# The experts' up projection with the tokens of both batches in one pass over the weights

## The chip, the core and the metric

The kernel runs on one core of a Trainium2 chip. A core has several engines that run at the same time, each through its own list of instructions in order: TensorE (PE in the profile) for matrix products, VectorE (DVE), ScalarE (ACT) and GpSimdE (POOL) for everything done element by element, and SyncE (SP), which here only starts transfers. Engines wait for each other through semaphores. TensorE works in pairs of instructions: LDWEIGHTS loads a stationary piece of 128 x 128, shown as PEld, and MATMUL streams up to 512 columns past it and adds the result into a PSUM bank. Eight banks of PSUM stand beside the main on-chip memory, SBUF.

The metric is the time of one execution on the device, in microseconds; lower is better.

## The reference

x has 2 batches of 512 tokens with 1024 features. The first part is a residual around a product of the normalized x with a context, both rounded to 256 levels. The second part, which the change touches, is a mixture of experts with a shared gated MLP:

```python
x = x + tanh(g_xattn) * (fake_quant(layernorm(x)) @ fake_quant(ctx))
xt = layernorm(x)
# gate: the two best of 16 experts per token, within the two best of 4 groups
y = 0
for e in experts:
    h = silu(xt @ w1[e] + b1[e]) * (xt @ w2[e] + b2[e])     # 1024 -> 256
    y = y + gate[:, e] * (h @ w3[e] + b3[e])                # 256 -> 1024
z = (silu(xt @ sw1 + sb1) * (xt @ sw2 + sb2)) @ sw3 + sb3   # hidden size 512
x = x + tanh(g_ffn) * (y + z)
```

## The kernel before

Everything is in float32 quality. A large product is made of three products in a faster float32 format (fp32r): each operand is split into a high half (`h` at the end of a name, or XH) and a low half (`l`, or XL), and the result is high x high + high x low + low x high. The token tiles count from t=0 to 7, four for each batch.

The kernel has four stages. In the first, up to about 106 us, x is normalized, quantized, multiplied with the context and normalized again, and transposed into XH and XL; part of the shared MLP's hidden layer is worked in between. This stage is written as a list of steps in a fixed order (START). In the second the rest of the shared hidden layer is made, with the router between its parts. In the third comes the shared down projection. In the fourth, from 200 us on, the two experts that the inputs choose, one after the other, each with an up projection and a down projection. A program that chose more experts would run the others in a loop behind it; that loop is not entered here.

An expert's hidden layer has 256 columns, worked in two blocks `c` of 128 (`expert`, L670). For a block, `load_up` (L308) starts two transfers of 512 KB, for the first and the second matrix (tiles named e0a0r, e0b0r: expert 0, matrix a or b, block 0, raw). `split_up` (L316) makes their halves: ACT copies the raw tile into the high half (L302), and DVE subtracts to get the low half (L304). Then `up` (L342) works on batch 0 and after it on batch 1. `up_mm` (L319) takes one matrix after the other. For a matrix it runs 24 products of 512 columns into one PSUM bank: eight row pieces of the high weights with XH, the same eight with XL, then the eight low pieces with XH. `up_post` (L333) makes the batch's hidden values: ACT's Silu of the first bank (L337), DVE's multiplication with the second (L338), ACT's cast to the high half (L339) and DVE's subtraction for the low half (L340). In the second block the expert's output bias, times the gate, is added to X by DVE in eight instructions (L386), in the program ahead of the block's products.

The down projection (`load_down` L345, `down` L366) loads and splits two tiles of w3 (e0d0r and e0d1r), and then takes the token tiles one after the other. For a tile and a block it runs six products of 512 columns: four with the tile's high hidden piece (high and low weights, for each half of the output columns, L372 and L373) and two with the low hidden piece (L375). DVE adds the result times the gate to X (L378). In the second expert each tile is stored when it is done; the last tile is done and stored in three column pieces (`down_last`).

Outside of START nobody writes the order of the instructions by hand. The framework's planner lays it down when the program is built: it goes through the program with estimated durations, decides on each engine which instruction comes next, and gives each tile a place from its pool. All weights in work, the hidden values and the biases come from one pool of 22 places of 4 KB a partition, PSUM's banks from a pool of six:

```python
slabs = ctx.enter_context(tc.tile_pool(name="slabs", bufs=22))
ps_mm = ctx.enter_context(tc.tile_pool(name="ps_mm", bufs=6, space=bass.MemoryType.PSUM))
```

What the planner laid down is then the fixed order in which each engine works, whatever the real durations are; each transfer is started by SP as soon as its place is free.

Of the kernel before, what the change touches and what calls it, by code (L numbers as in the profile page):

```python
# [19 lines left out]
D = 1024  # L20
KD = D // P
B = 2
# [12 lines left out]

# the order in which the start's loads and steps are issued, each step as function.arguments
LOADS = "x.1 x.3 c.0 c.1 x.2 c.2 c.3 c.4 c.5 c.6 c.7.0 c.7.1 w.1.1 x.4 b w.1.0 w.0.1 x.5 w.0.0"
# [40 lines left out]
def flamingo_block(  # L78
# [3 lines left out]
    nc = tc.nc  # L82
# [19 lines left out]

# [1 line left out]
    sc_in = const.tile([P, 6], F32, name="sc_in")  # L104
    nc.sync.dma_start(sc_in, scal.partition_broadcast(P))

# [1 line left out]
    X = [keep.tile([P, D], F32, name=f"X{t}") for t in range(NT)]  # L108

    # the engine that starts the DMAs; the paths that are rarely taken use GpSimd's queue  # L110
    dq = [nc.sync]
# [5 lines left out]

# [1 line left out]
    mhalf = const.tile([P, 1], F32, name="mhalf")  # L119
# [12 lines left out]
    nc.vector.tensor_scalar(nz, sc_in[:, 0:4], -1.0, None, ALU.mult)  # L132
    # zero points that bf16 holds exactly, less any quantized value, are integers of 0..255
    z8 = const.tile([P, 4], U8, name="z8")
# [25 lines left out]

# [1 line left out]
    def bn(t, h):  # L162
# [49 lines left out]

# [1 line left out]
    c8_, raws, qT, cq, acc = {}, {}, {}, {}, {}  # L214
# [21 lines left out]

# [1 line left out]
    sq_, md_, xn_, px_ = {}, {}, {}, {}  # L238

    def e(t, h):  # L240
        """The residual and its sum."""
        if h == 0:
            sq_[t] = [small.tile([P, 2], F32, name=f"{n}{t}", tag=n, bufs=4) for n in "sq"]
        xs = X[t][:, half(h)]
        nc.vector.scalar_tensor_tensor(  # L245
            xs, acc[t][h], cx_scale, xs, ALU.mult, ALU.add, accum_out=sq_[t][0][:, h : h + 1]
        )

    def sq(t, h):
        """H^2 times the squared deviations from the mean of half a row, H values."""  # L250
        if h == 0:
            xn_[t] = slab(f"xn{t}", F32)
        s, q = sq_[t]
        nc.scalar.activation(  # L254
            xn_[t][:, half(h)], X[t][:, half(h)], AF.Square,
            bias=s[:, h : h + 1], scale=-float(H), accum_out=q[:, h : h + 1],
        )

    def fm(t, eng):
        """The mean, and what the difference of the halves' means adds to the variance."""  # L260
        s, eng = sq_[t][0], pick(eng)
        d = small.tile([P, 1], F32, name=f"d{t}", tag="d", bufs=4)
        eng.tensor_tensor(d, s[:, 0:1], s[:, 1:2], ALU.subtract)
        eng.tensor_scalar(d, d, d, H / 2.0, ALU.mult, ALU.mult)
        nm = small.tile([P, 1], F32, name=f"nm{t}", tag="nm", bufs=4)
        eng.tensor_scalar(nm, s[:, 0:1], s[:, 1:2], -1.0 / D, ALU.add, ALU.mult)
        md_[t] = nm, d
# [38 lines left out]

# [1 line left out]
    def load_up(name, w1, w2, c):  # L308
# [10 lines left out]
    def up_mm(name, c, b, w, lo=0, n=S, i=(0, 1)):  # L319
# [11 lines left out]
        return got  # L331

    def up_post(name, c, b, acc, b1, b2, hid, lo=0, n=S):  # L333
        hh, hl = hid
        out = slice(b * S + lo, b * S + lo + n)
        sa = small.tile([P, S], F32, name=f"{name}sa{c}_{b}_{lo}", tag="w2k", bufs=3)[:, :n]
        nc.scalar.activation(sa, acc[0], AF.Silu, bias=b1)  # L337
        nc.vector.scalar_tensor_tensor(sa, acc[1], b2, sa, ALU.add, ALU.mult)  # L338
        nc.scalar.copy(hh[:, out], sa)  # L339
        nc.vector.tensor_tensor(hl[:, out], sa, hh[:, out].bitcast(F32), ALU.subtract)  # L340
# [12 lines left out]
    def down_last(name, t, hid, w3, scale):  # L353
        """A tile in column pieces, each stored as soon as it is done."""
        n = len(hid)
        for lo, w in ((0, 512), (512, 256), (768, 256)):
            cols = slice(lo, lo + w)
            po = bank(f"{name}po{t}_{lo}")[:, :w]
            for c, ((hh, hl), (wh, wl)) in enumerate(zip(hid, w3)):
                nc.tensor.matmul(po, hh[:, ts(t, P)], wh[:, cols], start=c == 0, stop=False)  # L360
                nc.tensor.matmul(po, hh[:, ts(t, P)], wl[:, cols], start=False, stop=False)
                nc.tensor.matmul(po, hl[:, ts(t, P)], wh[:, cols], start=False, stop=c == n - 1)
            nc.vector.scalar_tensor_tensor(X[t][:, cols], po, scale, X[t][:, cols], ALU.mult, ALU.add)
            dq[0].dma_start(of[ts(t, P), cols], X[t][:, cols])
# [22 lines left out]

    # ================= program =================
    XH, XL = ([keep.tile([P, KD, S], F32R, name=n), None] for n in ("XH0", "XL0"))
# [40 lines left out]

# [1 line left out]
    bT = const.tile([P, NB], F32, name="bT")  # L432
# [5 lines left out]

    # TensorE's clock is low until it has been busy for a few microseconds
    zero = const.tile([P, S], BF16, name="zero")  # L440
# [8 lines left out]

    # biases of the hidden layers, as columns  # L450
    def pb():
# [5 lines left out]

    # shared weights, split: half h of the rows of matrix i, hidden columns c
    def wh(c, i, h, eng):
# [8 lines left out]

    # hidden columns c of tokens lo..lo+255: matrix i, pass p of three
    def um(c, lo, i, p):  # L470
# [38 lines left out]

    # router weights, padded to the columns of a quarter of TensorE, and constants of the router  # L510
    rwf = const.tile([P, KD, QC], F32, name="rwf")
# [15 lines left out]
    def stage(b):  # L527
        """The buffers of a batch's attention."""
        qT[b] = keep.tile([P, TB, KD, P], BF16, name=f"qT{b}", tag="xh1")
        cq[b] = keep.tile([P, KD, D], BF16, name=f"cq{b}", tag="xl1")  # L530
# [12 lines left out]

# [1 line left out]
    def rt(name, shape=(P, NT, E), dtype=F32):  # L545
# [6 lines left out]
    def router_x(b):  # L552
        """The normalized x, transposed, in one float32 piece."""
        xs = []
        for i in range(4):
            x = slab(f"xf{b}_{i}", F32, (P, 2, S))
            nc.gpsimd.tensor_tensor(  # L557
                x, XH[b][:, ts(i, 2)].bitcast(F32), XL[b][:, ts(i, 2)].bitcast(F32), ALU.add
            )
            xs.append(x)  # L560
        return xs

    # the four quarters of TensorE's columns work at the same time, each on a fourth of the rows of D
    def router_logits(b, lT, xs):
# [19 lines left out]
    def first_max(name, v, n):  # L584
        """One-hot of the first largest of the last n."""
        m = rt(f"{name}m", (P, NT))
        nc.vector.tensor_reduce(m, v, AX.X, ALU.max)
        o = rt(f"{name}o", (P, NT, n))
        nc.vector.tensor_tensor(o, v, over(m, n), ALU.is_equal)
        order = tie[:, E - n :].unsqueeze(1).to_broadcast([P, NT, n])  # L590
        nc.vector.tensor_mul(o, o, order)
        nc.vector.tensor_reduce(m, o, AX.X, ALU.max)
        nc.vector.tensor_tensor(o, order, over(m, n), ALU.is_equal)
        return o

    # of all experts some token chose: 16 - e; of the others: 0
    key = route.tile([P, E], F32, name="key")
# [48 lines left out]
    def next_expert(j):  # L646
        """Of the chosen experts left, the one of lowest index: its index, gates and hidden biases."""
        m = rt(f"m{j}", (P, 1))
# [19 lines left out]

# [1 line left out]
    def expert(j, e, gv, bv, store):  # L670
        wc = lambda w: (lambda c: w[ds(e, 1), :, ts(c, P)].rearrange("o (k p) n -> p (o k) n", p=P))
        hid = []
        for c in range(EC):
            w = split_up(f"e{j}", c, load_up(f"e{j}", wc(ew1), wc(ew2), c), nc.vector)
            hid.append(new_hid(f"e{j}h{c}"))
            if c == EC - 1:
                bb = load_bias(f"e{j}", eb3[ds(e, 1), :].rearrange("o d -> (o d)").partition_broadcast(P))
                for t in range(NT):
                    add_bias(t, bb, gv[:, t : t + 1])
            for b in range(B):  # L680
                up(f"e{j}", c, b, w, bv[:, 0, c : c + 1], bv[:, 1, c : c + 1], hid[c])
        w3 = load_down(f"e{j}", lambda c: ew3[ds(e, 1), ts(c, P), :].rearrange("o p d -> (o p) d"), range(EC))
# [20 lines left out]

    # the rest of the shared MLP's hidden layer, with the router in between
    lT = slab("lT", F32)
# [21 lines left out]

# [1 line left out]
    def attention_exact(b):  # L729
# [64 lines left out]

# [1 line left out]
    n_exp = nc.values_load(n_chosen[0:1, 0:1], min_val=2, max_val=E)  # L796
# [54 lines left out]
```

## Time and profile before

| what | value |
|---|---|
| time, median of three runs | 344.21 us (344.01 to 344.89) |
| span of the profiled execution | 342.9 us |
| TensorE, matrix products | 321.7 us busy, 94% of the span, 1673 products |
| TensorE, weight loads | 254.5 us busy, 1673 loads |
| DVE, ACT, POOL | 197.0, 95.4 and 79.0 us busy |
| up projection of an expert | 192 products, 44.98 us |
| down projection of expert 0 | 245 to 267 us |
| bytes moved | 31.45 MB, mean 92 GB/s |

The profile has no total of its own beside the span for the profiled execution; the span runs from the first to the last instruction of the program, and the timed runs are 1.3 us longer at the median. A row of the timeline gives start and length in us, engine, line, operation, the tiles (result first, then operands) and the number of instructions merged in it; in brackets stands how long the engine had been idle before, and what ended the wait. The length of a product is its latency: products overlap, so the rate is read from their starts. "Busy" of TensorE counts that latency too.

### The profile page before, as it was taken

The numbers are of one execution on the slowest core, as the hardware profiler recorded it, in microseconds if no ns is written. First come the engines' busy times: TensorE is split into PE (matmuls) and PEld (weight loads), VectorE is DVE, ScalarE is ACT, GpSimd is POOL, SyncE is SP. The second block draws the span as 40 slices with busy tenths as digits, with TensorE's granted clock in tenths as the row PEclk, the third lists the DMA queues.
The fourth block names the chain that finished last, engine by engine and source line by source line (L and its number), as shares of the span: only waits on it lengthen the run. The fifth ranks groups of instructions, "written<-read, shape, count | busy, mean of one in ns | idle before, by whom it ended". The sixth has DMA issues, their size and how long they took to land.

```text
span 342.9 us, 4322 instructions
## 1 busy us (share of the span) xinstructions
PE 321.7 (94%) x1673; PEld 254.5 (74%) x1673; DVE 197.0 (57%) x335; ACT 95.4 (28%) x148; POOL 79.0 (23%) x110
## 2 busy tenths in 40 slices
PE   6588899989999999999999999999999999999990
PEld 2244886769998686888888888888888888888870
DVE  3879999879723126736754632494484135834560
ACT  2756877672213135120200002112400012030000
POOL 2795798868600740000000000000000000000000
PEclk9899999999999999999999999999999999999997
DMA  6999920000004033101200091201310400001542
GB/s 207 420 375 391 399 62 0 2 0 2 0 2 123 9 118 122 63 0 59 66 0 0 8 329 33 62 2 32 90 61 2 122 0 2 0 0 50 198 183 74
DMA packets 25892, 31.45 MB, mean 92 GB/s; under 512 B 2492, under 2 KB 19204, under 8 KB 25860
## 3 DMA queue, kind: packets, MB, share of 16 engines
q1 hardware_dynamic: 25860, 31.05, 26.5%
q8 instruction: 17, 0.28, 0.3%
q14 instruction: 15, 0.12, 0.1%
HBM read 26.85 MB, written 4.19 MB: 91 GB/s over the span
## 4 chain that ended last, share of the span: by engine, by line
PE 75%; DVE 8%; POOL 5%; ACT 4%; issue 3%; DMA 2%; SPq 0%; DVEq 0%; POOLq 0%
PE sp L327 16%; PE e1p L327 13%; PE e0p L327 13%; PE sp L476 5%; PE spo L373 4%; PE spo L372 4%; PE spo L375 4%; ACT xn L254 2%; PE e0po L372 2%; PE e0po L373 2%; PE e0po L375 2%; PE e1po L373 2%; PE e1po L372 2%; PE e1po L375 2%; DVE xn L283 2%
## 5 line engine op out<-in xcount | busy, mean ns | idle before, releaser
L233 PE MATMUL at<-cq,qT 128*128 128x512 bf16 x128 | 30.3, 379 | 2.5 <-POOL cq L153 1.5
L557 POOL TENSOR_TENSOR xf<-XH,XL 128x1024 f32<-128x1024 f32 x8 | 19.9, 2497 | 22.4 <-PE sp L327 19.6
L233 PEld LDWEIGHTS <-qT 128*128 128x128 bf16 x128 | 12.1, 98 | 15.5 <-issue 2.9
L378 DVE SCALAR_TENSOR_TENSOR X<-spo,tg,X 128x512 f32<-128x512 f32 x16 | 11.3, 746 | 16.0 <-PE spo L375 16.0
L338 DVE SCALAR_TENSOR_TENSOR ssa<-sp,bT,ssa 128x512 f32<-128x512 f32 (+1 forms) x6 | 4.0, 662 | 26.1 <-PE sp L327 26.1
L337 ACT ACTIVATE e0sa<-e0p,bv 128x512 f32<-128x512 f32 x4 | 2.8, 690 | 49.4 <-PE e0p L327 49.4
L378 DVE SCALAR_TENSOR_TENSOR X<-e0po,gv,X 128x512 f32<-128x512 f32 x16 | 11.3, 747 | 7.3 <-PE e0po L375 7.3
L283 DVE TENSOR_SCALAR xn<-X,nm,d 128x512 f32<-128x512 f32 x16 | 13.8, 891 | 1.4 <-POOL d L279 1.3
L378 DVE SCALAR_TENSOR_TENSOR X<-e1po,gv,X 128x512 f32<-128x512 f32 x14 | 9.9, 747 | 8.2 <-PE e1po L375 8.2
L288 PE MATMUL px<-ident,xn 128*128 128x128 f32 x64 | 9.3, 275 | 3.5 <-DVE xn L283 2.3
L337 ACT ACTIVATE e1sa<-e1p,bv 128x512 f32<-128x512 f32 x4 | 2.8, 690 | 34.9 <-PE e1p L327 34.9
L338 DVE SCALAR_TENSOR_TENSOR e1sa<-e1p,bv,e1sa 128x512 f32<-128x512 f32 x4 | 3.0, 752 | 15.9 <-PE e1p L327 15.9
L254 ACT ACTIVATE xn<-X,s 128x512 f32<-128x512 f32 x16 | 11.4, 716 | 1.9 <-DVE X L245 1.4
L245 DVE SCALAR_TENSOR_TENSOR X<-at,cx_scale,X 128x512 f32<-128x512 f32 x16 | 11.6, 742 | 0.1
L165 DVE BATCH_NORM_STATS2 st<-X 128x6 f32<-128x512 f32 x16 | 10.3, 680 | 2.2 <-DMA X<-in_dram 2.2
L338 DVE SCALAR_TENSOR_TENSOR e0sa<-e0p,bv,e0sa 128x512 f32<-128x512 f32 x4 | 3.0, 751 | 14.6 <-PE e0p L327 14.6
L288 PEld LDWEIGHTS px<-ident,xn 128*128 128x128 f32 x64 | 7.2, 141 | 5.6 <-ACT XH L145 2.6
L298 DVE TENSOR_TENSOR XL<-px,XH 128x512 fp32r<-128x512 f32 x16 | 10.4, 679 | 0.8 <-ACT XH L145 0.8
L386 DVE SCALAR_TENSOR_TENSOR X<-sbias,tg,X 128x1024 f32<-128x1024 f32 x8 | 10.3, 1284 | 0.3
L153 POOL TENSOR_SCALAR cq<-q8c,nz 128x1024 bf16<-128x1024 uint8 (+1 forms) x8 | 10.0, 1250 | 1.0 <-DVE q8c L223 0.6
L208 PE MATMUL pq<-ident_b,qx 128*128 128x128 bf16 x64 | 5.4, 228 | 4.7 <-ACT qx L151 4.4
L386 DVE SCALAR_TENSOR_TENSOR X<-e1bias,gv,X 128x1024 f32<-128x1024 f32 x8 | 9.8, 1280 | 0.0
(402 smaller groups left out, 830.9 us busy)
## 6 DMA issues: line engine op xcount, KB each, us to landing
cr<-in_dram SPq DMA_DIRECT2D x15, 512.0 KB, 9.2
out_dram<-X SPq DMA_DIRECT2D x15, 256.0 KB, 2.4
X<-in_dram SPq DMA_DIRECT2D x7, 512.0 KB, 9.0
X<-in_dram SPq DMA_DIRECT2D x2, 256.0 KB, 4.1
cr<-in_dram SPq DMA_DIRECT2D x2, 256.0 KB, 9.1
sb1r<-in_dram SPq DMA_DIRECT2D x1, 512.0 KB, 9.0
sa1r<-in_dram SPq DMA_DIRECT2D x1, 512.0 KB, 7.2
sb0r<-in_dram SPq DMA_DIRECT2D x1, 512.0 KB, 8.2
```

The lines of the kernel that those rows point to most:

```text
L233: nc.tensor.matmul(acc[t][h], qT[b][:, t % TB, k, :], cq[b][:, k, half(h)], start=(k == 0), stop=(k == KD - 1))
L254: nc.scalar.activation(xn_[t][:, half(h)], X[t][:, half(h)], AF.Square, bias=s[:, h : h + 1], scale=-float(H), accum_out=q[:, h : h + 1],)
L283: nc.vector.tensor_scalar(xn_[t][:, half(h)], X[t][:, half(h)], nm, r, ALU.add, ALU.mult)
L288: nc.tensor.transpose(px_[t, q][:, k, :], xn_[t][:, ts(4 * q + k, P)], ident)
L327: nc.tensor.matmul(p, wx[:, k, :], xx[b][:, k, cols], start=first and k == 0, stop=last and k == KD - 1)
L372: nc.tensor.matmul(po[h], hh[:, ts(t, P)], wh[:, ts(h, 512)], start=first, stop=False)
L373: nc.tensor.matmul(po[h], hh[:, ts(t, P)], wl[:, ts(h, 512)], start=False, stop=False)
L375: nc.tensor.matmul(po[h], hl[:, ts(t, P)], wh[:, ts(h, 512)], start=False, stop=last)
L378: nc.vector.scalar_tensor_tensor(xs, po[h], scale, xs, ALU.mult, ALU.add)
L386: nc.vector.scalar_tensor_tensor(X[t], bb, scale, X[t], ALU.mult, ALU.add)
L476: nc.tensor.matmul(up_[c, lo, i], w[:, k, :], x[0][:, k, lo : lo + 256], start=p == 0 and k == 0, stop=p == 2 and k == KD - 1,)
L557: nc.gpsimd.tensor_tensor(x, XH[b][:, ts(i, 2)].bitcast(F32), XL[b][:, ts(i, 2)].bitcast(F32), ALU.add)
```

## The change

Only the experts' up projection changes. A new function `up_both` takes the two matrices in turn. For a matrix it opens two banks, one for each batch, and goes through the eight row pieces once. At each it runs four products with the high weight piece (batch 0 with XH and XL, batch 1 with XH and XL) and then two with the low weight piece (batch 0 and batch 1 with XH). `expert` calls it once for a block and then calls `up_post` for batch 0 and for batch 1. The number of products, loads, banks, transfers and of the instructions in `up_post` stays what it was. The shared MLP keeps `up`. The diff also takes comments away; nothing else differs.

```diff
+    def up_both(name, c, w):
+
+        got = [[], []]
+        for i in range(2):
+            ps = [bank(f"{name}p{c}_{b}_{i}") for b in range(B)]
+            for k in range(KD):
+                for b in range(B):
+                    for j, xx in enumerate((XH, XL)):
+                        nc.tensor.matmul(
+                            ps[b], w[i][0][:, k, :], xx[b][:, k, :], start=k == 0 and j == 0, stop=False
+                        )
+                for b in range(B):
+                    nc.tensor.matmul(ps[b], w[i][1][:, k, :], XH[b][:, k, :], start=False, stop=k == KD - 1)
+            for b in range(B):
+                got[b].append(ps[b])
+        return got
+
...
     def expert(j, e, gv, bv, store):
...
+            both = up_both(f"e{j}", c, w)
             for b in range(B):
-                up(f"e{j}", c, b, w, bv[:, 0, c : c + 1], bv[:, 1, c : c + 1], hid[c])
+                up_post(f"e{j}", c, b, both[b], bv[:, 0, c : c + 1], bv[:, 1, c : c + 1], hid[c])
```

## The prediction

> **What bounds the kernel now.** I read the page's busy rows and its chain first, then the chain in order of time, then TensorE's timeline, and last the timelines of ACT, DVE and the DMA queue around the experts. The page:
>
> ```profile
> span 342.9 us, 4322 instructions
> PE 321.7 (94%) x1673; PEld 254.5 (74%) x1673; DVE 197.0 (57%) x335; ACT 95.4 (28%) x148; POOL 79.0 (23%) x110
> PEclk9899999999999999999999999999999999999997
> PE sp L327 16%; PE e1p L327 13%; PE e0p L327 13%; PE sp L476 5%; PE spo L373 4%; PE spo L372 4%; PE spo L375 4%; ACT xn L254 2%; PE e0po L372 2%; PE e0po L373 2%; PE e0po L375 2%; PE e1po L373 2%; PE e1po L372 2%; PE e1po L375 2%; DVE xn L283 2%
> ```
>
> TensorE sets the time, at the full granted clock, and each expert's up projection (e0p, e1p) is 13% of the chain. Every MATMUL has its own LDWEIGHTS (1673 of each), so a repeated piece is loaded again. The chain in order of time (start and length in us, as in the timelines below) shows both up projections without a gap:
>
> ```profile
> 200.13 44.98 PE e0p L327 x192
> ...
> 266.87 44.98 PE e1p L327 x192
> ```
>
> 44.98 us over 192 products is **234.3 ns** a product. TensorE's timeline of the down projection gives the starts of two tiles that follow each other:
>
> ```profile
> 247.67 0.39 PE L372 MATMUL e0po<-e0d0h,e0h0h 128*128 128x512 f32 x1
> ...
> 250.39 0.39 PE L372 MATMUL e0po<-e0d0h,e0h0h 128*128 128x512 f32 x1
> ```
>
> 12 products in 2.72 us: **226.7 ns** each, for products of the same size and type (the 0.39 is one product's latency, and they overlap).
>
> **The gain.** `up` does eight pieces of the high half with XH, the same eight with XL, then eight low pieces, so the piece changes at every product. `up_both` uses each high piece for four products (two into one bank, two into the other) and each low piece for two. That is the order of `down`: hh four times over two banks, hl twice. So I take the down row, the nearest: 2 x 192 x (234.3 - 226.7) ns = **2.9 us** saved. The ends: nothing, if the 234.3 comes from something else[...]. Against them: for 256 columns the up rows run at 118.9 ns and the last down tile's at 120, so reuse there bought nothing.
>
> **The cost: when the hidden units come out.** Of a block of hidden columns (`c`), batch 0 was finished half-way, 11.2 us before the block's end. Now both batches' gate banks finish half-way and both banks of the second matrix at the end. Two Silu on ACT stay at the middle; STT (L338), cast (L339) and subtraction (L340) of both batches fall behind the block's last product. What else is ordered behind them? ACT and DVE work through the order that the planner wrote. The DMA queue's timeline:
>
> ```profile
> 132.93 0.33 SPq L349 DMA_DIRECT2D sd3r<-in_dram  x1
> ...
> 195.62 0.38 SPq L312 DMA_DIRECT2D e0a1r<-in_dram  x1
> ...
> 237.64 0.37 SPq L312 DMA_DIRECT2D e1a1r<-in_dram  x1
> ```
>
> and ACT's:
>
> ```profile
> 146.05 0.62 ACT L339 CAST sh3h<-ssa 128x512 fp32r<-128x512 f32 x1 [5.84 <-DVE ssa L338]
> 146.57 1.05 ACT L302 CAST sd3h<-sd3r 128x1024 fp32r<-128x1024 f32 x1
> ...
> 212.26 0.62 ACT L339 CAST e0h0h<-e0sa 128x512 fp32r<-128x512 f32 x1 [5.79 <-DVE e0sa L338]
> 212.79 1.05 ACT L302 CAST e0a1h<-e0a1r 128x1024 fp32r<-128x1024 f32 x1
> ...
> 279.01 0.62 ACT L339 CAST e1h0h<-e1sa 128x512 fp32r<-128x512 f32 x1 [5.73 <-DVE e1sa L338]
> 279.54 1.05 ACT L302 CAST e1a1h<-e1a1r 128x1024 fp32r<-128x1024 f32 x1
> ```
>
> Those loads take 3.4 to 4.0 us, so the weights had landed about 10, 13 and 38 us before their casts, and ACT was idle for 5.7 to 5.8 us just before. Yet each cast stands right behind the cast of batch 0's hidden units. In the program that cast is the first writer of a slab, and these weights are asked for later. The row of DMA slots fits: e0a1r, e0bias, e0d0r, e0d1r and e1a0r start as the last shared down tile lets go of slabs, spaced as if every slab between them (e0a1h to e0d1l, with e0h1h ahead of e0d0r) were given out in program order. I conclude that **the planner gives out slabs strictly in program order of their first writers**, so in its plan weights that come after a block's hidden units load only once these begin. The real load is early; only the place in ACT's and DVE's order is late. Before, that place was half-way through a block, 10 us ahead of need. Now it is behind the block's end: at c=0 stand behind it the weights of c=1 (a1, b1), at c=1 those of the down projection (d0, d1). Nothing of this is on POOL, and SP's DMAs keep number and order. TensorE, first in need of them, waits.
>
> **The wait, step by step**, u being when TensorE would start its next product. The rows are the two starts of TensorE and DVE at a unit's end, then the two of DVE behind:
>
> ```profile
> 233.69 2.04 PE L327 MATMUL e0p<-XH,e0a1h 128*128 128x512 f32 x8
> 233.96 0.75 DVE L338 SCALAR_TENSOR_TENSOR e0sa<-e0p,bv,e0sa 128x512 f32<-128x512 f32 x1 [1.59 <-PE e0p L327]
> ```
>
> ```profile
> 212.91 0.69 DVE L340 TENSOR_TENSOR e0h0l<-e0sa,e0h0h 128x512 fp32r<-128x512 f32 x1 [0.69 <-ACT e0h0h L339]
> 213.87 1.23 DVE L304 TENSOR_TENSOR e0a1l<-e0a1r,e0a1h 128x1024 fp32r<-128x1024 f32 x1 [0.26 <-ACT e0a1h L302]
> ```
>
> STT starts 0.27 behind the next product; batch 0's last product is now one earlier (0.23): u+0.04. The two STT take 1.41 together (as L378's pairs do), to u+1.45. The cast starts 0.79 after its STT (234.75 against 233.96): u+0.83, to 1.45; batch 1's at u+1.49. The next cast starts 0.53 later (212.79 - 212.26): a1h from u+2.02, 1.05 long, to 3.07. Its low half starts 0.03 later, 1.23 long, to u+4.33; the two L340 (0.69 each) fit before. TensorE resumes 0.15 after a release (px at 71.82 after xn, 70.90 + 0.77): u+3.22. The first low piece is its fifth product, due at 3.22 + 0.91 = 4.13, possible at 4.33 + 0.15 = 4.48: 0.35 more. So **3.6 us at c=0 to c=1**. At the down projection the second product already needs d0l: 4.48 against 0.23, **4.2 us**. d1 comes after d0 (d1h to 4.1, d1l to 5.6; due 5.8), no more. Four waits: 2 x (3.6 + 4.2) = 15.6 us. Behind the waiting casts on ACT stand b1h or d1h, which have slack; on DVE b1l and the eight bias additions (9.8 us, in a block of 22: hidden).
>
> Costed at nothing: the earlier need of low pieces at each expert's first block (e1a0l is done at 250.2, needed at 267.8); Silu of both batches together; PSUM (four banks a block, as before, and the next block's pair finds Silu's long done).
>
> **The clock** [...] it speaks against the change. The row: TensorE idle for 4.4 us at 6.8, then
>
> ```profile
> 11.00:14.40 3.40, 3.22 (x13) 1.50 (x14) 2.70 (x6) 3.03 (x5) 2.82 (x8) 0.50 1.02 418
> ```
>
> the clock (0.50, ahead of the DMA share) is halved for 3.4 us; no shorter idle time (1.2 at most) did that. [...] My gaps are 3.1 us, with a lone product before the last 1.0 of the down ones: by the row unproven[...]. I take 0; if each gap trips it, half of 3.4 us four times, 6.8 us.
>
> **Sum**: 15.6 - 2.9 = +12.7 us on the span of 342.9, 355.6. What lies outside the span, 1.3 us against the median of 344.21, stays: **356.9 us**.
>
> **Rivals.**
> - A: waits as above, products stay at 234.3: 344.2 + 15.6 = 359.8. For it: the 256-column rows. Against: the order equals that of down.
> - B, faster: the planner puts a1h and d0h ahead of the hidden casts, as it put sd0h and sd1h (125.98, 126.92) ahead of the cast of sh2h (131.80), which comes first in the program (but there the slab of sh2h had had its first writer long before). Then only the first down tile waits: its seventh product, due at u+1.36, needs the hidden cast (1.45 + 0.15): 0.24 an expert. 344.2 - 2.9 + 0.5 = 341.8. It decides if the four waits average under 0.7 us. Against: three casts of weights asked for later, none ahead.
> - B with no gain in rate: 344.7, within the noise.
> - C: only one kind of block boundary waits: 344.2 - 2.9 + 7.2 to 8.4 = 348.5 to 349.7.
> - D: the clock trips as well: 358.6 to 363.7.
>
> **How the numbers follow.** Mine 0.60, A 0.17, B 0.08, B without gain 0.02, C 0.07, D 0.06. Range 348 to 361.5: it leaves out both B and the upper part of D, and its top is A with a tripped clock. Faster 0.08, within 0.3% (about what this kernel's measurement can tell from no change) 0.02, slower 0.90.
>
> **What would show it.** Chain: 192 products in 43.5 us without the waits. PE's waits: ACT e0a1h and e0d0h some 3 us each, then DVE's low halves. ACT's order: hidden cast, hidden cast, weight cast, behind the last product. Wrong if ACT casts a1h in the middle of the block, or if products still come every 234 ns.

## The result and the profile after

The changed kernel takes 364.76 us at the median of four runs (364.10 to 365.17), against 344.55 (344.01 to 345.58) for the kernel before in the same comparison. The ratio is **1.058, with a 95% interval of 1.056 to 1.060**: 20.2 us slower. The prediction was 356.9 us with a range of 348 to 361.5. The direction and the main cause hold; the size does not, and the time lies 3.3 us above the range.

The page of the profile after, in the lines that answer to those shown of before:

```profile
span 362.8 us, 4324 instructions
PE 328.0 (90%) x1673; PEld 256.5 (71%) x1673; DVE 195.9 (54%) x335; ACT 94.9 (26%) x148; POOL 78.9 (22%) x110
PEclk9899999999999999999999999899899999998996
PE sp L327 16%; PE e0p L341 9%; PE e1p L341 8%; PE sp L493 4%; PE e0p L345 4%; PE e1p L345 4%; PE spo L389 4%; PE spo L390 4%; PE spo L392 4%; PE e0po L390 2%; ACT xn L254 2%; PE e0po L392 2%; PE e1po L390 2%; PE e0po L389 2%; DMA X<-in_dram 2%
```

The products and loads are as many as before. TensorE's share fell from 94% to 90% of a span that is 19.9 us longer, and the row of the granted clock has three new dips (8) in its later half. The chain in order of time (start, length, what) shows where the first of the lost time lies:

```profile
200.42 0.93 PE e0p L341 x4
201.35 0.47 PE e0p L345 x2
...
222.97 0.48 issue
223.44 0.75 DVE e0sa L355
224.22 0.62 ACT e0h0h L356
224.84 0.96 ACT e0a1h L302
225.84 1.45 PE e0p L341 x4
227.29 1.03 PE e0p L345 x2
```

Two readings. Six products (four with a high piece, two with a low one) take 1.40 us: still some **234 ns** each, although each piece is now used four times or twice in a row. And at the block's end the chain leaves TensorE for DVE's product, ACT's cast of the hidden values and, behind it, ACT's cast of the next weights. After that gap the four products take 1.45 us in place of 0.93.

What TensorE waited for (total, times, longest, in us), in the experts:

```profile
PE e1po L389 <- ACT e1d0h L302: 2.9, 1, 2.9
PE e1p L341 <- ACT e1a1h L302: 2.9, 1, 2.9
PE e0po L389 <- ACT e0d0h L302: 2.9, 1, 2.9
PE e0p L341 <- ACT e0a1h L302: 2.9, 1, 2.9
...
PE e0po L390 <- DVE e0d0l L304: 0.5, 1, 0.5
...
PE e1po L390 <- DVE e1d0l L304: 0.2, 1, 0.2
```

These are the four waits that the prediction named. ACT's timeline around the first of them:

```profile
211.46 1.27 ACT L354 ACTIVATE e0sa<-e0p,bv 128x512 f32<-128x512 f32 x2 [44.39 <-PE e0p L345]
223.56 1.28 ACT L356 CAST e0h0h<-e0sa 128x512 fp32r<-128x512 f32 x2 [10.83 <-DVE e0sa L355]
224.74 1.04 ACT L302 CAST e0a1h<-e0a1r 128x1024 fp32r<-128x1024 f32 x1
225.69 1.05 ACT L302 CAST e0b1h<-e0b1r 128x1024 fp32r<-128x1024 f32 x1
```

ACT had been idle for 10.83 us, in which it could have made e0a1h, whose transfer SP had issued at 195.92. The last product of the block started at about 222.5.

What the prediction left at nothing is in the stretches of 3.41 us ahead of and behind each gap (columns: stretch, its length, busy time of PE, PEld, DVE, ACT, POOL, the granted clock, then DMA share and GB/s):

```profile
223.20:226.61 3.41, 0.78 (x3) 0.68 (x4) 3.13 (x5) 3.01 (x4) 0.00 (x0) 1.00 0.00 0
226.61:230.02 3.41, 3.41 (x9) 2.35 (x8) 3.41 (x4) 0.13 (x1) 0.00 (x0) 0.50 0.01 2
250.50:253.91 3.41, 0.73 (x2) 0.30 (x2) 3.13 (x5) 2.99 (x4) 0.00 (x0) 1.00 0.00 0
253.91:257.33 3.42, 2.92 (x7) 2.34 (x8) 1.59 (x2) 2.03 (x3) 0.00 (x0) 0.50 0.00 0
298.30:301.70 3.40, 1.54 (x7) 0.92 (x5) 1.97 (x3) 1.17 (x3) 0.00 (x0) 1.00 0.00 0
301.70:305.12 3.42, 2.29 (x9) 1.59 (x10) 3.17 (x5) 1.97 (x3) 0.00 (x0) 1.00 0.02 5
325.60:329.01 3.41, 0.47 (x3) 0.23 (x2) 3.00 (x5) 2.46 (x4) 0.00 (x0) 1.00 0.01 2
329.01:332.42 3.41, 3.21 (x8) 1.99 (x8) 2.12 (x2) 0.67 (x1) 0.00 (x0) 0.50 0.01 2
```

Behind three of the four gaps the clock is halved (0.50) for 3.41 us, and products come every 427 ns there. From the start of an earlier halving (11.57 to 14.98, clock 0.50) to those of these three (226.61, 253.91 and 329.01 us) it is 63, 71 and 93 times 3.413 us: in this profile they lie on a fixed grid. A stretch of the grid in which TensorE was busy for 0.47 to 0.78 us was followed by a halving; at the fourth gap, as long as the others, the grid cuts the idle time in two, TensorE is busy for 1.54 and 2.29 us in the two parts, and no halving follows.

The experts' stages from first product to first product, in us (the last ends with the last product on e1po):

| stage | before | after | after with products in the gaps (first experiment) |
|---|---|---|---|
| expert 0, block 0 | 22.48 | 25.58 | 25.59 |
| expert 0, block 1 | 22.49 | 27.32 | 26.02 |
| expert 0, down | 21.77 | 24.03 | 21.88 |
| expert 1, block 0 | 22.49 | 25.58 | 25.59 |
| expert 1, block 1 | 22.49 | 26.02 | 26.02 |
| expert 1, down | 21.72 | 23.73 | 21.84 |

The six stages are 18.8 us longer. Another 0.3 us lies ahead of the experts and 0.8 us behind them, in parts that the change does not touch; I have not traced these to a cause.

### The profile page after: what moved, and what is told of

It is laid out like the page before. It is cut to its first block, busy times and chain, and to the rows that moved or that the text cites. A ratio compares the mean times of both kernels' runs of the same rounds, so it can differ in the third digit from the quotient of the medians.

```text
span 362.8 us, 4324 instructions
## 1 busy us (share of the span) xinstructions
PE 328.0 (90%) x1673; PEld 256.5 (71%) x1673; DVE 195.9 (54%) x335; ACT 94.9 (26%) x148; POOL 78.9 (22%) x110
## 4 chain that ended last, share of the span: by engine, by line
PE 72%; DVE 9%; POOL 5%; ACT 5%; issue 4%; DMA 2%; SPq 0%; DVEq 0%; POOLq 0%
PE sp L327 16%; PE e0p L341 9%; PE e1p L341 8%; PE sp L493 4%; PE e0p L345 4%; PE e1p L345 4%; PE spo L389 4%; PE spo L390 4%; PE spo L392 4%; PE e0po L390 2%; ACT xn L254 2%; PE e0po L392 2%; PE e1po L390 2%; PE e0po L389 2%; DMA X<-in_dram 2%
## 5 line engine op out<-in xcount | busy, mean ns | idle before, releaser
L233 PE MATMUL at<-cq,qT 128*128 128x512 bf16 x128 | 30.3, 379 | 2.4 <-POOL cq L153 1.5
L574 POOL TENSOR_TENSOR xf<-XH,XL 128x1024 f32<-128x1024 f32 x8 | 19.9, 2499 | 22.2 <-PE sp L327 19.4
L233 PEld LDWEIGHTS <-qT 128*128 128x128 bf16 x128 | 12.1, 98 | 15.4 <-issue 2.8
L151 ACT ACTIVATE qx<-q8x,nz 128x1024 bf16<-128x1024 uint8 (+1 forms) x7 | 7.2, 1023 | 9.8 <-DVE q8x L197 9.8
```

What stands on the lines that cost most here:

```text
L233: nc.tensor.matmul(acc[t][h], qT[b][:, t % TB, k, :], cq[b][:, k, half(h)], start=(k == 0), stop=(k == KD - 1))
L574: nc.gpsimd.tensor_tensor(x, XH[b][:, ts(i, 2)].bitcast(F32), XL[b][:, ts(i, 2)].bitcast(F32), ALU.add)
```

## The experiments

Four questions: does the clock cost what is missing, does the order of the planner's slabs make the waits, why do products still come every 234 ns, and is anything left to gain.

**1. The clock.** Twelve products that nobody uses, into a bank of their own, fill the gap behind each block. They keep TensorE busy and delay nothing that the gap would not have delayed.

```diff
             both = up_both(f"e{j}", c, w)
+            pf = tbank(f"e{j}f{c}")
+            for k in range(12):
+                nc.tensor.matmul(pf, w[1][0][:, k % KD, :], XH[0][:, k % KD, :], start=k == 0, stop=k == 11)
```

> The changed kernel with twelve more products of 512 columns behind each block of the up projection (results used by nobody), so that TensorE has work during the wait and its clock has no reason to fall. They take 12 x 234 ns = 2.8 us, less than the 3.3 us between the last product before the wait and the first after it. Clock theory (three halvings of the clock cost some 5 us on top of the waits): the granted clock stays at 1.00 in the experts' stage, the waits stay, time 344.4 + 15.5 = 359.9 us. Rival (the halved clock lies in time that is lost anyway, the waits are simply longer than worked out): 364.8 us or more.

Measured: 359.17 us (358.01 to 359.46), ratio 1.040 (1.037 to 1.042). The experts' time in one stretch, with the columns as above:

```profile
200.00:350.00 150.00, 147.34 (x635) 117.80 (x633) 66.86 (x78) 19.54 (x26) 0.00 (x0) 1.00 0.19 67
```

The clock is 1.00 throughout, against 0.97 in the changed kernel. The work added made the kernel 5.6 us faster. In the table above, the stages behind the gaps at 226, 254 and 329 us lose 1.30, 2.15 and 1.89 us of their length, and the stage behind the gap that tripped nothing (expert 1, block 1) loses none. Of the 2.15 and 1.89, 0.52 and 0.2 us are the waits on DVE's e0d0l and e1d0l; here six products with the high weights stand ahead of the first with a low half, which covers them. That leaves 1.3 + 1.6 + 1.7 = **4.6 us for the clock**, and 14.2 us for the waits. The whole times agree: 359.17 us is 14.1 above the kernel before as it was timed beside this run (345.04).

**2 to 4. Where the operands lie.** Products of the same size come every 234.3 ns in an up projection and every 226.7 in a down projection, in both orders of the pieces. My next idea was the place of the operands within 64 bytes: in the program as built, XH and XL lie 160 bytes past a multiple of 512, and the slabs (the places of the common pool, where the weights lie) at one. Two edits shift them. The first moves both XH, XL and the slabs; with the second, both are on multiples of 64.

```diff
-    tg = const.tile([P, 2], F32, name="tg")
+    tg = const.tile([P, 16], F32, name="tg")[:, :2]
...
-    key = route.tile([P, E], F32, name="key")
+    key = route.tile([P, E + 8], F32, name="key")[:, :E]
```

The first edit alone, in the kernel before:

> The kernel before with one constant made 32 bytes longer, so that every later place in SBUF moves by 32 bytes: XH and XL (they start 32 bytes past a multiple of 64) come to start at a multiple of 64, and the slabs, which started at one, come to start 32 past it. Place theory (a product's rate depends on whether its moving rows start at a multiple of 64 bytes): the up products change from 234.3 to 226.7 ns and the down products from 226.7 to 234.3; 2 x 192 + 192 up products of 512 columns gain 4.4 us, 384 down products lose 2.9 us, time 344.4 - 1.5 = 342.9 us. Rival (something in the up projection itself sets the rate: eight different pieces, the accumulation into one bank, the tiles' shape): both rates stay, 344.4 us.

Measured: 345.25 us, ratio 1.001 (1.000 to 1.003), and both rates unchanged (234.3 and 226.8 ns). Both edits in the kernel before:

> The kernel before with two tiles made 32 bytes longer, so that XH, XL and the slabs all start at a multiple of 64 bytes. Place theory: up and down products both at 226.7 ns, time 344.4 - 4.4 = 340.0 us. Rival (the up projection itself sets its rate): 344.4 us.

Measured: 343.99 us, ratio 0.998 (0.996 to 0.9995). An up projection takes 44.79 us in place of 44.98, which is 233.3 ns a product. Both edits in the changed kernel:

> The changed kernel with the same two tiles 32 bytes longer. Place theory: up products at 226.7 ns whatever the order of pieces; the waits and about three halvings of the clock stay; time 364.8 - 4.4 = 360.4 us, within 1.7 us for each halving more or less. If repeating a piece has a value of its own which the place had covered, its products come faster than those of the kernel before with the same places. Rival: 234.3 ns and 364.8 us.

Measured: 366.87 us, ratio 1.063 (1.059 to 1.067), no faster than the changed kernel itself. Its gaps are the same 2.9 us, but they fall differently on the grid: all four are followed by a halving, and one halving lasts for two stretches, so that five stretches are halved rather than three.

So the place within 64 bytes is not it: with everything aligned the rate is nearly what it was. But the second edit, which alone changes the *distance* between XH and the slabs, changed the rate; the first, which moves both together, did not. That pointed to the next question.

**5. The waits.** If the planner gives out slabs in program order of their first writers, an early first writer of the hidden slabs frees the weights behind them. GpSimd, which has nothing to do in this stage, writes one column of each hidden tile ahead of the block's products; the real values overwrite it.

```diff
+            for h in hid[c]:
+                nc.gpsimd.memset(h[:, :1].bitcast(F32), 0.0)
             both = up_both(f"e{j}", c, w)
```

> The changed kernel with one addition: ahead of a block's products GpSimd sets the first column of the block's two hidden tiles to zero (it is written over later). The order of everything else in the program stays, but the first writer of these slabs now comes ahead of the products. Slab theory (the planner gives out slabs in program order of their first writers, and that put the casts of the next weights behind the block's end): ACT's casts e0a1h, e0d0h, e1a1h, e1d0h stand ahead of the blocks' ends, the four waits vanish down to 0.2 us an expert, products stay at 234 ns, time 344.8 us. Rival (the planner puts a cast of hidden units ahead of a later weight cast by rank, whatever the slabs): the order on ACT and the 364.8 us stay.

Measured: 345.52 us (344.50 to 346.40), ratio 1.003 (1.001 to 1.005): 19 of the 20 us are gone. ACT's timeline:

```profile
200.00 1.05 ACT L302 CAST e0a1h<-e0a1r 128x1024 fp32r<-128x1024 f32 x1 [32.56 <-DMA e0a1r<-in_dram]
...
205.69 1.06 ACT L302 CAST e0d0h<-e0d0r 128x1024 fp32r<-128x1024 f32 x1 [2.86 <-DMA e0d0r<-in_dram]
211.52 1.27 ACT L354 ACTIVATE e0sa<-e0p,bv 128x512 f32<-128x512 f32 x2 [4.78 <-PE e0p L345]
212.68 1.05 ACT L302 CAST e0d1h<-e0d1r 128x1024 fp32r<-128x1024 f32 x1
223.61 1.22 ACT L356 CAST e0h0h<-e0sa 128x512 fp32r<-128x512 f32 x2 [9.87 <-DVE e0sa L355]
```

The next block's weights (e0a1h) are now cast at 200.00, as block 0 begins; in the changed kernel that cast came at 224.74, behind block 0's hidden values. Those of the down projection (e0d0h, e0d1h) are cast during block 0, ahead of its hidden values; in the changed kernel they came behind those of block 1. TensorE has no wait of note in the experts. Up blocks take 22.48 us again, as before the change. The down projections take 22.1 us, 0.35 more than before: the seventh product of the first tile waits a little for the hidden cast, as rival B had it (0.24).

**6. The same cure in program order.** The next weights' loads and splits are written ahead of `up_post`, and no instruction is added.

```diff
+        get = lambda c: split_up(f"e{j}", c, load_up(f"e{j}", wc(ew1), wc(ew2), c), nc.vector)
+        w = get(0)
         for c in range(EC):
-            w = split_up(f"e{j}", c, load_up(f"e{j}", wc(ew1), wc(ew2), c), nc.vector)
...
             both = up_both(f"e{j}", c, w)
+            if c < EC - 1:
+                w = get(c + 1)
+            else:
+                w3 = load_down(f"e{j}", lambda c: ew3[ds(e, 1), ts(c, P), :].rearrange("o p d -> (o p) d"), range(EC))
             for b in range(B):
                 up_post(f"e{j}", c, b, both[b], bv[:, 0, c : c + 1], bv[:, 1, c : c + 1], hid[c])
-        w3 = load_down(f"e{j}", lambda c: ew3[ds(e, 1), ts(c, P), :].rearrange("o p d -> (o p) d"), range(EC))
```

> The changed kernel with the loads and splits of the next weights (block 1 behind block 0, w3 behind block 1) written in the program ahead of up_post. Slab theory: as in the run with the early first writer, no waits of microseconds at the block's ends, 344.8 us. By the order of the program alone both theories expect that, so this run is the price of the cure, not a test between them; if TensorE still waits for ACT's casts, both are wrong.

Measured: 345.72 us (343.99 to 346.73), ratio 1.002 (1.0005 to 1.004), blocks of 22.49 us, no waits. This shows the price of a cure without a dummy write; it does not tell the two theories apart, as its expectation says. The test between them is experiment 5.

**7. What sets the rate.** In place of the experts' up products, 16 streams of 24 products run in the kernel before, each stream varying one thing: whether the piece changes, whether the moving rows change, whether they lie in XH or in a slab, one bank or two. `sw` is a piece of the high weights, `sx` a piece of XH, `mx`, `mo` and `mw` moving rows of XH, of the other batch's XH and of a slab:

```python
s, m = {
    0: lambda: (sw(k), mx(k)),
    1: lambda: (sw(0), mx(k)),
    2: lambda: (sw(k), mx(0)),
    3: lambda: (sw(0), mx(0)),
    4: lambda: (sw(k), mw(n % 2)),
    5: lambda: (sw(0), mw(n % 2)),
    6: lambda: (sw(0), mw(0)),
    7: lambda: (sx(k), mw(n % 2)),
    8: lambda: (sx(k), mo(k)),
...
```

> The kernel before with its sixteen groups of 24 products of the experts' up projection replaced by sixteen streams that differ in where the stationary piece and the moving rows lie and in which of them repeat (the hidden units are then not the reference's; all else runs as before). Read is the time from product to product in each. Piece theory: fast (227 ns) where the piece repeats (streams 1, 3, 5, 6, 9, 11, 12), slow (234) where it changes. Moving-side theory: fast where the moving rows lie in slabs (4, 5, 6, 7, 11, 12), slow where they lie in XH or XL, whatever the piece. Bank theory: fast where two banks take turns (10, 11), slow else. If several of these are mixed, the rate follows the two addresses together.

Measured, in four of the timeline's rows (behind the arrow first the moving tile, then the one that holds the piece) and a table:

```profile
200.29 5.78 PE L371 MATMUL cp<-XH,e0a0h 128*128 128x512 f32 x24
205.91 5.79 PE L371 MATMUL cp<-XH,e0b0h 128*128 128x512 f32 x24
...
222.78 5.62 PE L371 MATMUL cp<-e0b1h,e0a1h 128*128 128x512 f32 x24
228.24 5.60 PE L371 MATMUL cp<-e0a1h,e0b1h 128*128 128x512 f32 x24
```

| streams | piece | moving rows | ns a product |
|---|---|---|---|
| 0, 1 | slab: changing, or always the same | XH | 234.3 |
| 2, 3 | slab: changing, or always the same | one row piece of XH | 234.1 |
| 10 | slab, changing, two banks in turn | XH | 234.1 |
| 15 | slab, changing | XL | 234.3 |
| 4, 5, 6 | slab: changing, the same, all fixed | slab | 226.6 |
| 11, 12 | slab, the order of `down`, two banks or one | slab | 226.7 |
| 7 | XH, changing | slab | 233.6 |
| 8, 9 | XH: changing, or fixed | the other batch's XH | 226.7 |
| 13, 14 | slab, changing | XH, 8 or 16 values further on | 233.3 |

From the first stream to the second 5.62 us pass, 24 x 234.2 ns; the fifth starts 5.46 before the sixth, some 227. Whether the piece repeats makes no difference: streams 0 and 1 agree, and 4 and 5 agree. Neither does the bank. It is not the moving tile alone either, for XH with XH runs at the fast rate and a slab with XH pieces at the slow one. In these streams, both operands in the same region go with the fast rate and operands in different regions with the slow one.

**8. Region or distance.** In the same place, the moving rows start some values further on, so that their distance from the piece, modulo 512 bytes, takes chosen values (160 is the kernel's own, in XH).

```python
if far:
    m = flat(XH[b])[:, 512 * (n % 7) + o : 512 * (n % 7) + o + 512]
else:
    m = flat(w[1 - i][0])[:, o : o + 512]
nc.tensor.matmul(p, w[i][0][:, n % KD, :], m, start=n == 0, stop=n == 23)
```

> As the run with sixteen streams, with the stationary piece always in a slab and changing at every product, and the moving rows either in XH (streams 0 to 8) or in a slab (9 to 15), begun some values behind the row's start (the hidden units are not the reference's). In the built program XH lies 160 bytes past a multiple of 512 and the slabs at one, so the distance of the moving rows from the piece, modulo 512 bytes, is 160, 256, 384, 480, 496, 0, 16, 32, 0 for streams 0 to 8 and 0, 16, 32, 64, 128, 160, 256 for 9 to 15. Distance theory (products come at 226.6 ns where this distance is 0 and slower elsewhere): 5, 8 and 9 fast, all others at 230 to 238. Region theory (what counts is that both lie in the same region of SBUF): 9 to 15 fast, 0 to 8 slow.

Measured, timeline rows and table (rates are those inside a stream):

```profile
200.81 5.78 PE L348 MATMUL cp<-XH,e0a0h 128*128 128x512 f32 x24
206.43 5.61 PE L348 MATMUL cp<-XH,e0b0h 128*128 128x512 f32 x24
...
277.81 5.72 PE L348 MATMUL cp<-e1b0h,e1a0h 128*128 128x512 f32 x24
```

| distance modulo 512 | moving rows in XH, ns | in a slab, ns |
|---|---|---|
| 0 | 226.7 | 226.7 |
| 16 | 231.7 | 231.7 |
| 32 | 233.3 | 233.4 |
| 64 | | 228.9 |
| 128 | | 232.2 |
| 160 | 234.3 | 234.1 |
| 256 | 226.6 | 226.6 |
| 384 | 233.3 | |
| 480 | 233.3 | |
| 496 | 226.7 | |

The three rows are XH at the kernel's own distance (160), XH at 256, and a slab moved by 16 bytes. At the five distances tried in both regions (0, 16, 32, 160, 256) the two agree within 0.2 ns, so it is the distance that counts and not the region. One pair fits less well: at 128 the slab came at 232.2, while XH at that distance, in experiment 3, came at 233.3; why is open. A distance of 256 is as fast as 0; and 496, 16 bytes below a multiple, is fast while 16 above is not. I had expected neither, nor the 228.9 at 64. With this the earlier runs make sense: the first edit of experiment 2 left the distance at 160, both edits together made it 128 modulo 512, and up projections ran at 234.3 and 233.3 ns.

**9. The distance put right in the kernel before.** 160 more bytes ahead of the slabs, nothing else:

```diff
-    key = route.tile([P, E], F32, name="key")
+    key = route.tile([P, E + 40], F32, name="key")[:, :E]
```

> The kernel before with one tile of the router made 160 bytes longer, so that the slabs, which lie behind it, come to lie 160 bytes past a multiple of 512 as XH and XL do. Distance theory: all up products at 226.6 ns, down products unchanged, 576 products of 512 columns gain 7.7 ns each, time 344.8 - 4.4 = 340.4 us. Region theory: 344.8 us.

Measured: **340.63 us** (339.77 to 340.85), ratio 0.987 (0.983 to 0.990). Its chain in order of time:

```profile
198.67 43.52 PE e0p L327 x192
...
263.95 43.52 PE e1p L327 x192
```

192 products in 43.52 us are 226.7 ns each, in the old order of the pieces. The two up projections give 2 x 1.46 = 2.9 us, exactly the gain that the prediction had put down to the order; and the experts also start 1.5 us earlier. The shared MLP's products of 256 columns gained nothing: their longest series (135 products, from 90 us on) goes from 118.7 to 120.0 ns a product. This one edit beats both kernels.

**10. The new order with both cures.** The changed kernel with the early first writer of experiment 5 and the 160 bytes:

> The changed kernel with the early first writer of the hidden slabs and the same 160 bytes: no waits, and, by the distance theory, all products at 226.6 ns: 345.5 - 4.4 = 341.1 us. By the region theory 345.5 us. Against the kernel before with the 160 bytes it shows what the new order of products is worth by itself: nothing is expected, apart from the 0.3 us per expert that the first down tile waits.

Measured: 341.08 us (340.55 to 342.68), ratio 0.989 (0.986 to 0.992). Its chain:

```profile
199.15 0.91 PE e0p L341 x4
200.05 0.45 PE e0p L345 x2
```

Six products in 1.36 us: 226.7 ns, as in experiment 9. The up blocks of both take 21.76 us; the down projections are 22.10 and 22.04 us here and 21.76 and 21.71 there. The new order buys nothing even when nothing stands in its way, and costs some 0.35 us an expert. The two totals themselves are too close to be told apart.

## Why the prediction was right and wrong

**The waits: place, cause and nearly the size.** "The planner gives out slabs strictly in program order of their first writers" was read from the weights' casts standing behind the hidden casts while ACT had been idle. Experiment 5 adds only an earlier first writer, and the casts move ahead and the waits go, so it is shown that the first writer's place makes the waits; that the rule is *strict*, for every slab, was not tried. Rival B, in which the planner casts the weights early, fell. Against the working: TensorE's standstill from u was worked out as 3.22 us and measured 3.10 each time (the stages of block 0 grew by that); a1's low half was 0.35 and measured 0.43 (26.02 - 22.49 - 3.10). The term "at the down projection the second product already needs d0l" was mis-sized: 1.0 more was put down, and 0.6 and 0.3 came (0.5 and 0.2 in TensorE's waits, and 0.1 that experiment 1 shows too). I had assumed the old order in the first down tile; the planner put two products with d0h ahead of the first with d0l. In sum 4 x 3.10 + 0.9 + 0.9 = 14.2 us in place of 15.6.

**The gain: wrong.** The step that failed is "so I take the down row, the nearest". That row differed from the up row in two things, the order of the pieces and the place of the moving operand, and I looked at the first alone. Measured: 0 in place of 2.9 us; "products still come every 234 ns", which the prediction had named as a sign of being wrong, came true. Stream 0 against stream 1 shows that the order of the pieces is worth nothing: 234.3 ns both where the piece changes at every product and where it is always the same. The fp32r products of 512 columns came no faster than 226.6 ns in any stream or order; the bf16 products of the context in the first stage of the kernel before (L233, also 512 columns) follow each other at 215 to 216 ns. Evidence against me was in my own text: the 256-column rows showed no gain from reuse. They could not have pointed to the distance either, as experiment 9 shows (118.7 to 120.0 ns). Rival A took it, at a chance of 0.17.

**The clock: wrong.** "I take 0" rested on the row, in which 4.4 us of idle time tripped the halving and 1.2 us did not. My gaps (3.1) lie between the two; that they would trip nothing was my estimate, and the row did not show it. I looked only at the *length* of a gap. In the trace the halvings lie on a grid of 3.41 us, and three of four gaps shorter than that tripped it: stretches in which TensorE was busy for 0.47 to 0.78 of 3.41 us were followed by a halving, and one with 1.54 was not. So a stretch need not be wholly idle. Measured: 4.6 us in place of 0, inside the bound of 6.8 that I had named. Where a bound is that large and the row leaves the gap between 1.2 and 4.4 us open, zero was no value "by the row".

**The range** failed with these two together. Rival A lay inside it and rival D in part (up to 363.7), but A (359.8) *with* a tripped clock came out, and the range's top of 361.5 held A with one halving only (359.8 + 1.7), not with three. From 356.9: +2.9 for the gain, +4.6 for the clock, -1.4 for the waits, +1.1 ahead of and behind the experts, +0.7 between the profiled span and the median (2.0 us against 1.3 before) gives 364.8, the measured median. That last 0.7 is no cost of the change: in every run that lists both, the time is 1.6 to 1.8 us above its own span, and each median was set against the span of another execution.

**What was costed at nothing and was nothing:** b1h, d1h and the bias additions behind the waits, both Silu together, PSUM, the low pieces of the first block. In experiment 5, where the waits are gone, blocks take 22.48 us, as in the kernel before.

## What to carry to other kernels

When work is regrouped so that results come out together at a block's end, look at what stands *behind* those results in each engine's order: here it was the next weights' casts, kept there only by the order in which places in the pool are given out, and an earlier first writer or load moved them. Price an idle gap of TensorE with the clock included, by the share of a stretch of the 3.41-us grid that it can leave idle (here stretches with 0.47 to 0.78 us of busy time were followed by a halving, one with 1.54 us was not) and not by its own length. And before a difference in rate is put down to the order of the instructions, compare everything else in which the two rows differ, addresses too.

## What the runs showed of the hardware that was not expected

- In experiments 3 and 7 to 10 the rate of fp32r products of 512 columns went with the distance in SBUF between the moving rows and the stationary piece: 226.6 ns at a multiple of 256 bytes and 16 below one, 228.9 to 234.3 at the other distances tried. With 256 columns no such gain was seen (118.7 ns at a distance of 160, 120.0 at 0). Changing or repeated pieces and one bank or two made no difference. In this kernel 160 bytes of padding are worth 4 us, 1.3% (344.75 to 340.63 us, experiment 9). All pieces of a stream have the same place modulo 512, so the runs cannot say whether it is the piece in use or the next one being loaded that counts; what lies underneath was not tried.
- In the profile after, the clock was halved (0.50) for 3.41 us after stretches of a 3.41-us grid in which TensorE had been busy for up to 0.78 us, and was not halved after one with 1.54 us. The profile before agrees: a halving follows the idle stretch from 7.59 us and the one from 335.27 us, and none follows the least busy of the others (1.84 us of busy time, from 331.85 us). Neither profile has a stretch with a busy time between 0.78 and 1.54 us, so where the turn lies was not shown. The same gap of 2.9 us costs 1.3 to 1.7 us more or nothing, by where it falls on the grid, and about 3.2 us where the halving lasted for two stretches (expert 0's down projection in experiment 4: 25.59 us against 21.88, less a wait of 0.5). Where the grid stands against the program's start differed from profile to profile (the first halving starts at 11.00 us in that of before and at 11.57 us in that of after), and the changed kernel's four runs have mean clocks of 0.965 to 0.974; so the number of halved stretches may well differ between executions of one kernel, and the five in experiment 4 need not come from its shifted operands.
- At the half clock (0.50), fp32r products of 512 columns came every 427 ns in up and down projections alike (profile after, from 226.61 and 329.01 us); the difference between 234.3 and 226.7 is gone there.
